# A two-block decoder on one core: PSUM split four and four, and seven-product first multiplications in four more expert layers

## The chip, the cores and the metric

The kernel runs on one core of one Trainium2 chip. The metric is device microseconds of one execution. Each kernel is timed in several runs; the profile is one more execution, taken by the hardware profiler. Engines are named as in the profile: PE multiplies matrices (PEld is its weight load), DVE, ACT and POOL work on vectors, SP starts most of the DMAs. PSUM, into which PE writes and which DVE and ACT read, has eight banks of 128 x 512 float32.

## The reference

Sixteen sequences of 128 rows of 256 features go through two blocks, all in float32. Every sublayer ends with `x = layernorm(x + sublayer(x))`.

```
block 0: causal attention, 16 heads of 64, over groups of 512 rows
         8 ensembles: o_e = relu(x @ in_e) @ out_e, summed with gates   (256 -> 512 -> 256)
         routed experts, best 2 of 16, and 2 shared ones
block 1: banded attention, 16 heads of 16
         cross attention to ctx_512, 16 heads of 16
         8 experts: y_e = gelu(x @ w1_e + b1_e) @ w2_e + b2_e, summed   (256 -> 512 -> 256)
```

In block 0 the gates of the eight ensembles come from an integer tensor and the context. In block 1 every expert works on every row, and the sum is scaled by one gate for each row. The change concerns the two layers of eight dense experts, which are called expert layers here, and where attention scores are put.

## The kernel before

**Groups.** The 16 sequences are worked in four groups of four, g = 0 to 3, of 512 rows each. A sublayer of one group is one stage, written as (number, g): 0 is causal attention (`attention0`), 1 the ensembles (`ensemble0`), 2 the routed experts (`experts0`, for two groups at once), 3 banded attention, 4 cross attention (both through `attention16`), 5 the dense experts of block 1 (`experts1`). There are eight expert layers: (1, 0) to (1, 3) and (5, 0) to (5, 3).

**Order of the work.** Every stage is a Python generator that emits instructions and yields an estimate of the PE time it has just emitted. The `Weaver` (L217 to L257) takes pieces from a main stream of attention stages and a side stream of dense stages, L1462, in shares given by hand (L1466 to L1472), with short streams for normalisation, gates, routing and loads in between. The first attention stages (0, 0) and (0, 1) run alone, then attention and experts run woven together, and the last two expert layers (5, 2) and (5, 3) run alone. A scheduler then orders instructions by that emission order as their operands and buffers come free, and gives every tile a buffer at build time; the program of each engine is fixed before it runs.

**PSUM.** `bank(tag)`, L49, takes a bank from one pool of six (tag "B"), whatever the tag in its name: psH, psM and psO in the profile all come from this pool. Attention scores, psS, have a tile of two banks of their own, tag "S" with one buffer (L424 in causal attention, L520 in the 16-head attention). In causal attention the DVE instruction L352 reads the scores once into SBUF. In banded attention L352 does too; in cross attention two DVE instructions read them from PSUM, L358 (the maximum) and L364 (its subtraction). The next scores wait until the last reader is done. After the softmax POOL multiplies by the reciprocal of the sum (L380), PE transposes (L60), ACT copies (L390), and PE multiplies with the values into psO.

**An expert layer.** `products` (L796) runs over nine steps. In step e the first products of expert e (`x @ in_e`, hidden layer of 512) are emitted in four pieces, and between them four pieces of the second products of expert e - 1. The second products always use the seven-product scheme for 2 x 2 blocks: four sums on DVE (L812 to L815), the blocks of the second weights summed by POOL beforehand (L696, L699) and kept in HBM, four banks psM and four additions into `acc` on DVE (L836).

**First products, plain.** A piece is one bank psH with two matmuls of 128 x 128 by 128 x 512 (`project`, L316), read by one instruction: L942 on DVE in block 0 (relu and gate), L1365 on ACT in block 1 (gelu and bias).

**First products by sevens** (class `Firsts`, L722), used before in (5, 2) and (5, 3) for experts 1 to 7. Expert 0 stays plain. Once for each layer DVE makes four block sums of the activations (`rows_sums`). For each expert POOL makes four sums of weight blocks, in place or in tag "cw" (`weight_sums`, L740, instructions L720 and L746). The seven products, 14 matmuls of 128 x 128 by 128 x 256, go partly into one running bank, `sums` (psH), which is read by ACT three times in between and keeps accumulating, and partly into `other` (psM):

```
            self.product(e, 5, sums)
            nc.scalar.copy(block(1, 0), sums)
            yield 0.91
            other = both(bank("M"))
            self.product(e, 4, sums)
            nc.scalar.copy(block(1, 1), sums)
            self.product(e, 3, other, start=True)
            added(1, 1, other)
            yield 1.82
            self.product(e, 2, other, stop=True)
            added(1, 0, other)
```

`added` is one DVE addition of 128 x 512 (L771); after it the block is finished by `done` (relu and gate, or two gelus).

**Tag "cw"** has four buffers, which `weight_sums` shares with the gate masks (L908, instruction L909), the routing plan and the collection of routed results (L1300).

Of the kernel before, what the change touches and what calls it, by code (L numbers as in the profile page):

```python
# [8 lines left out]
F32 = mybir.dt.float32  # L9
# [5 lines left out]
P = 128  # L15
D = 256
# [6 lines left out]
T = GB * P  # L23
# [8 lines left out]
def kernel(ctx: ExitStack, tc: tile.TileContext, a: dict, out: bass.AP):  # L32
# [11 lines left out]
    ps = ctx.enter_context(tc.tile_pool(name="psum", bufs=2, space=bass.MemoryType.PSUM))  # L44
# [2 lines left out]


    def bank(tag):  # L49
        return ps.tile([P, T], F32, tag="B", name=f"ps{tag}", bufs=6)  # L50

    recent = [None]

# [49 lines left out]
    def load_quad(j):  # L103

        cols = slice(j * D, (j + 1) * D)
        return load_w(
            "attn", 2048, f"wquad{j}", a["L0_attn_W_Q"][:, :, cols], a["L0_attn_W_K"][:, :, cols],
            a["L0_attn_W_V"][:, :, cols], a["L0_attn_W_O"][:, 2 * j:2 * j + 2, :],
        )
# [206 lines left out]
    def project(pt, w, cols, xT):  # L316

        for c in range(KC):
            mm(pt, lhsT=w[:, c, cols], rhs=xT[:, c, :], start=c == 0, stop=c == KC - 1)
# [76 lines left out]
    def attention0(x, g):  # L396
        norm = Norm(x)
        norm.bias(bo0)

        def project_quad(g, j):  # L400
            wq, wk, wv, wo = first_quads[j] if g == 0 and j < 2 else load_quad(j)
            xT = xTs[g]
            qT = p2.tile([P, 2, T], F32, tag="qT", name="qT")
            kT = p2.tile([P, 2, T], F32, tag="kT", name="kT")
            for i in range(2):
                c = 2 * j + i
                cols = slice(i * P, (i + 1) * P)
                pq = bank("H")
                project(pq, wq, cols, xT)
                nc.vector.tensor_scalar(  # L410
                    qT[:, i, :], pq, bq0[:, c:c + 1], 0.125, ALU.add, ALU.mult
                )
                pk = bank("H")
                project(pk, wk, cols, xT)
                nc.scalar.activation(kT[:, i, :], pk, AF.Identity, bias=bk0[:, c:c + 1])
                yield 3.44

            v = yield from values(xT, wv, KC)
            heads0[g, j] = qT, kT, v, wo

        def scores(j, b):
            qT, kT, _, _ = heads0[g, j]
            at = slice(b * P, (b + 1) * P)
            s = ps.tile([P, 2, T], F32, tag="S", name="psS", bufs=1)[:, :, :D].rearrange(  # L424
                "p s (i k) -> p s i k", i=2
            )

            for i in range(2):
                for k in range(2):
                    rows = slice(64 * k, 64 * k + 64)  # L430
                    with joined(i == k == 0):
                        mm(
                            s[:, k, i, :], lhsT=qT[rows, i, at], rhs=kT[rows, i, at],
                            start=True, stop=True,
                        )
            return softmax(s, causal)

        def output(j, b, zT):
            po = bank("H")[:, :D]
            for i in range(2):  # L440
                mm(po, lhsT=zT[:, i, :], rhs=heads0[g, j][3][:, i, :], start=i == 0, stop=i == 1)
            norm.add(b, po, last=j == 3)

        if (g, 0) not in heads0:
            yield from project_quad(g, 0)
        units = [(j, b) for j in range(4) for b in range(GB)]
        e, eT, zT, at = {}, {}, {}, {}
        for n in range(len(units) + 5):
            if n < 16:
                j, b = units[n]  # L450
                e[n] = scores(j, b)
                at["e", n] = weaver.now + 9.0
                yield 0.6
            m = n - 2
            if m in e:
                yield UNTIL, at["e", m]
                eT[m], _ = weights_T(e.pop(m))
                at["t", m] = weaver.now + 2.5
                yield 0.5
            m = n - 5  # L460
            if m in zT:
                yield UNTIL, at["z", m]
                output(*units[m], zT.pop(m))
                yield 0.86
            m = n - 4
            if m in eT:
                j, b = units[m]
                yield UNTIL, at["t", m]

                pz = bank("O")[:, :D].rearrange("p (c q) -> p c q", c=2)  # L470
                got = eT.pop(m)
                for i in range(2):
                    for k in range(2):
                        h = 2 * i + k
                        with joined(h == 0):
                            mm(
                                pz[64 * k:64 * k + 64, i, :],
                                lhsT=heads0[g, j][2][:, b, 64 * h:64 * h + 64],
                                rhs=got[:, 2 * k + i, :], start=True, stop=True,
                            )  # L480
                zT[m] = p3.tile([P, 2, P], F32, tag="z", name="zT")

                nc.vector.tensor_tensor(  # L483
                    zT[m], pz, bv0[:, 2 * j:2 * j + 2].unsqueeze(2).to_broadcast([P, 2, P]), ALU.add
                )
                at["z", m] = weaver.now + 2.5
                yield 0.6
            if n < 16 and (n < 12 or g + 1 < NG):

                j, b = units[n]  # L490
                if b == 0:
                    ahead = project_quad(g, j + 1) if j < 3 else project_quad(g + 1, 0)
                yield next(ahead)
                if b == 3:
                    assert next(ahead, None) is None
        assert not e and not eT and not zT
        norm.done()


    def attention16(x, qT, kT, v, bv, wo, bo, seen):  # L500
# [9 lines left out]
        def scores(b, c):  # L510

            at = slice(b * P, (b + 1) * P)

            kb = p2.tile([P, 4, P], F32, tag="kb", name="kb")
            nc.gpsimd.tensor_tensor(  # L515
                kb, kT[:, c, at].unsqueeze(1).to_broadcast([P, 4, P]),
                hm4.unsqueeze(2).to_broadcast([P, 4, P]), ALU.mult,
            )
            yield UNTIL, weaver.now + 2.0
            s = ps.tile([P, 2, T], F32, tag="S", name="psS", bufs=1)  # L520
            s = s[:, :, :4 * keys].rearrange("p s (h k) -> p s h k", h=4)
            for k in range(2):
                rows = slice(64 * k, 64 * k + 64)
                for queries, key, _ in parts:
                    mine = slice(b * P + queries.start, b * P + queries.stop)
                    with joined(k == 0 and key == 0):
                        mm(
                            s[queries, k], lhsT=qT[rows, c, mine],
                            rhs=kb[rows, :, key:key + keys], start=True, stop=True,
                        )  # L530
            return softmax(s, seen)
# [400 lines left out]
    def ensemble0(x, xT, g):  # L932
        def load(e):
            gt = p2.tile([P, T], F32, tag="sg", name="gt")
            nc.sync.dma_start(out=gt, in_=gates_of[g][e:e + 1, :].to_broadcast([P, T]))
            gates[e] = gt
            return load_up(f"we0_{e}", a["L0_xattn_proj_in"][e])[0]

        def hidden(h, up, e, c):
            ph = bank("H")  # L940
            project(ph, up, slice(c * P, (c + 1) * P), xT)
            nc.vector.scalar_tensor_tensor(  # L942
                out=h, in0=ph, scalar=0.0, in1=gates[e], op0=ALU.max, op1=ALU.mult
            )

        def done(to, got, e, i, j):
            gt = gates[e][:, j * 2 * P:(j + 1) * 2 * P]
            nc.vector.scalar_tensor_tensor(
                out=to, in0=got, scalar=0.0, in1=gt.unsqueeze(1).to_broadcast([P, 2, 2 * P]),
                op0=ALU.max, op1=ALU.mult,  # L950
            )

        gates = {}
        norm = Norm(x)
        yield from products(
            load, lambda e: load_blocks(0, e, g, a["L0_xattn_proj_out"][e]), hidden,
            lambda t: after(
                products_end(t, norm, None, lambda norm, b: norm.done(b, 2)), tail(1, g)
            ),
            Firsts(xT, done) if g in () else None,  # L960
        )

    def small(tag, n=16, bufs=None):
# [391 lines left out]
    def experts1(x, xT, g, ng):  # L1355
# [16 lines left out]
        for b in range(GB):  # L1372
# [4 lines left out]
        yield from products(  # L1377
            load, lambda e: load_blocks(1, e, g, a["L1_ffn_w2"][e]), hidden,
            lambda t: after(products_end(t, norm, ng, lambda norm, b: store(norm, g, b))),
            Firsts(xT, done) if g in (2,3) else None,  # L1380
        )


# [158 lines left out]
```

## Time and profile before

| | |
|---|---|
| time, median of 3 runs | 1738.57 us (1735.91 to 1738.95) |
| profiled execution, its own time | 1738.27 us |
| its span | 1736.6 us |
| mean granted PE clock | 0.975 |

The table shows busy us of each engine, in stretches cut at the ends of the expert layers (the last addition of a layer, L878, stands at 372.9, 538.9, 833.9, 1015.9, 1328.5, 1507.4, 1623.8 and 1721.9 us) and of the routed experts.

| from to, us | what runs | PE | DVE | ACT | POOL |
|---|---|---|---|---|---|
| 0 to 212 | (0, 0), (0, 1) | 203.1 | 117.6 | 93.0 | 96.5 |
| 212 to 539 | (1, 0), (1, 1) beside (0, 2), (0, 3) | 325.3 | 205.9 | 52.3 | 65.6 |
| 539 to 680 | routed experts, groups 0 and 1; rest of (0, 3) | 121.8 | 70.3 | 51.3 | 20.5 |
| 680 to 834 | (1, 2) beside attention | 150.9 | 123.8 | 24.6 | 46.3 |
| 834 to 1016 | (1, 3) beside attention | 176.6 | 152.2 | 40.6 | 52.3 |
| 1016 to 1150 | routed experts, groups 2 and 3, and attention | 114.4 | 86.2 | 52.4 | 44.1 |
| 1150 to 1328 | (5, 0) beside attention | 169.4 | 132.5 | 90.6 | 70.0 |
| 1328 to 1507 | (5, 1) beside attention | 173.8 | 131.9 | 93.0 | 56.6 |
| 1507 to 1736 | (5, 2), (5, 3) | 212.1 | 143.8 | 93.9 | 53.7 |

How to read it: matmuls are pipelined and the profile models their ends, so PE's busy time overstates what PE needs where passes overlap, and the start-to-start time of two records says what a pass costs. A float32 matmul stands as two records. Idle time of an engine that isn't the bound costs nothing. The slices of the page give the same picture over the span; each digit is a tenth of the slice:

```profile
PE   9999999999999799999899988998999999999996
...
DVE  4565565576677534878796875858769675965655
ACT  4434411111022242103131212643846372654342
POOL 5443532220002302312241315334224132522220
```

### The profile page before, as it was taken

What the parts mean: (1) busy time and instruction counts of PE and PEld (TensorE: products, weight loads), DVE (VectorE), ACT (ScalarE), POOL (GpSimd) and SP (SyncE); (2) the same over time, 40 slices, a digit from 0 to 9 for tenths busy, and PEclk for the clock granted to TensorE, in tenths of its full rate; (3) what the DMA queues carried; (4) which work ended last, traced back from release to release, by engine and by line L of the source; (5) the groups of instructions that cost most, each with busy time, mean ns of one, the idle gap of its engine ahead of it and who ended that gap; (6) DMA issues with size and microseconds to landing.
All of it is one profiled execution on the core that took longest, in us unless ns stands there. A gap on an engine that the chain in (4) does not pass through costs nothing.

```text
span 1736.6 us, 22830 instructions
## 1 busy us (share of the span) xinstructions
PE 1647.3 (95%) x8196; PEld 1080.5 (62%) x8196; DVE 1164.0 (67%) x2330; ACT 591.8 (34%) x1360; POOL 505.5 (29%) x543
## 2 busy tenths in 40 slices
PE   9999999999999799999899988998999999999996
PEld 6665656666656465656556655665665665588785
DVE  4565565576677534878796875858769675965655
ACT  4434411111022242103131212643846372654342
POOL 5443532220002302312241315334224132522220
PEclk9999999999998899999999989999999999999998
DMA  9533533432330458422223204671222221124330
GB/s 272 174 118 123 172 140 111 150 112 103 103 110 13 146 186 290 153 93 82 90 79 104 80 31 170 202 245 64 68 91 80 71 70 67 63 83 134 113 121 34
DMA packets 98192, 204.52 MB, mean 118 GB/s; under 512 B 16136, under 2 KB 58176, under 8 KB 98016
## 3 DMA queue, kind: packets, MB, share of 16 engines
q1 hardware_dynamic: 92176, 179.53, 31.2%
q0 software_dynamic: 5904, 23.54, 3.7%
q8 instruction: 65, 1.06, 0.2%
q14 instruction: 47, 0.39, 0.1%
HBM read 172.43 MB, written 37.81 MB: 121 GB/s over the span
## 4 chain that ended last, share of the span: by engine, by line
PE 75%; DVE 12%; DMA 4%; issue 3%; POOL 2%; ACT 1%; SPq 1%; another core or an unknown queue 0%; POOLq 0%; DVEq 0%; ACTq 0%
PE psH L55 40%; PE psM L55 21%; PE psO L60 5%; PE psS L55 4%; PE psO L55 3%; PE psH L60 2%; DVE nmax L358 1%; DVE e L364 1%; DMA wquad<-in_L_attn_W_Q 1%; DMA rows<-copies 1%; DVE total L370 1%; DVE x L311 1%; DVE x L293 1%; DVE acc L836 1%; POOL got L1303 1%
## 5 line engine op out<-in xcount | busy, mean ns | idle before, releaser
L55 PE MATMUL psH<-xT,we 128*128 128x512 f32 (+1 forms) x856 | 397.4, 590 | 0.5 <-DMA we<-in_L_xattn_proj_in 0.5
L380 POOL TENSOR_TENSOR e<-e,inv 128x512 f32<-128x512 f32 (+2 forms) x121 | 159.4, 1319 | 425.6 <-DVE inv L378 369.7
L55 PE MATMUL psM<-cm,wb 128*128 128x256 f32 x1024 | 263.6, 381 | 0.0
L55 PEld LDWEIGHTS psH<-xT,we 128*128 128x128 f32 x856 | 156.8, 191 | 137.0 <-issue 124.9
L55 PEld LDWEIGHTS psM<-cm,wb 128*128 128x128 f32 x1024 | 192.0, 190 | 52.2 <-issue 25.7
L55 PE MATMUL psM<-h,wb 128*128 128x256 f32 x768 | 200.8, 384 | 5.0 <-ACT h L1365 3.4
L836 DVE TENSOR_TENSOR acc<-psM,acc 128x512 f32<-128x512 f32 (+1 forms) x216 | 134.5, 624 | 98.3 <-PE psM L55 98.2
L390 ACT COPY eT<-psO 128x512 f32<-128x512 f32 (+1 forms) x192 | 105.5, 584 | 275.6 <-PE psO L60 261.3
L55 PEld LDWEIGHTS psM<-h,wb 128*128 128x128 f32 x768 | 143.0, 190 | 54.8 <-issue 29.3
L373 ACT ACTIVATE e<-e,nmax 128x128 f32<-128x128 f32 x256 | 99.5, 390 | 139.6 <-DVE nmax L358 113.4
L942 DVE SCALAR_TENSOR_TENSOR h<-psH,gt 128x512 f32<-128x512 f32 x128 | 87.6, 685 | 71.5 <-PE psH L55 71.2
L55 PE MATMUL psH<-xT,wquad 128*128 128x512 f32 x256 | 117.2, 601 | 6.1 <-DMA wquad<-in_L_attn_W_Q 5.4
L515 POOL TENSOR_TENSOR kb<-kT,hm 128x512 f32<-128x512 f32 x64 | 72.4, 1134 | 159.1 <-PE psS L55 104.5
L60 PEld LDWEIGHTS psO<-ident,e 128*128 128x128 f32 (+1 forms) x768 | 85.2, 133 | 48.2 <-issue 35.9
L60 PE MATMUL psO<-ident,e 128*128 128x128 f32 (+1 forms) x768 | 109.7, 280 | 2.0 <-POOL e L380 2.0
L1365 ACT ACTIVATE h<-psH,b 128x512 f32<-128x512 f32 (+1 forms) x100 | 60.6, 623 | 104.7 <-PE psH L55 95.9
L369 ACT ACTIVATE e<-e 128x576 f32<-128x576 f32 (+1 forms) x64 | 55.7, 871 | 88.2 <-DVE e L364 87.9
L55 PEld LDWEIGHTS psH<-xT,wquad 128*128 128x128 f32 x256 | 46.7, 190 | 58.9 <-issue 47.8
L309 POOL TENSOR_TENSOR rstd<-ve,mhalf 128x4 f32<-128x4 f32 (+1 forms) x32 | 28.9, 903 | 177.9 <-DVE ve L307 177.6
L370 DVE TENSOR_REDUCE total<-e 128x8 f32<-128x576 f32 (+1 forms) x64 | 62.8, 981 | 24.6 <-ACT e L369 24.0
L55 PE MATMUL psO<-eT,v 128*64 128x128 f32 (+2 forms) x1024 | 76.6, 313 | 0.0
L55 PE MATMUL psH<-wquad,zT 128*128 128x256 f32 x256 | 67.8, 388 | 4.8 <-DVE zT L483 2.5
(240 smaller groups left out, 2624.0 us busy)
## 6 DMA issues: line engine op xcount, KB each, us to landing
wb<-wbd SPq DMA_DIRECT2D x56, 896.0 KB
we<-in_L_xattn_proj_in SPq DMA_DIRECT2D x32, 512.0 KB
wt<-table SPq DMA_DIRECT2D x64, 256.0 KB
we<-in_L_ffn_w SPq DMA_DIRECT2D x32, 512.0 KB
wbd<-wb POOLq DMA_DIRECT2D x16, 896.0 KB
gt<-gatesd SPq DMA_DIRECT2D x32, 256.0 KB
results<-y SPq DMA_DIRECT2D x10, 768.0 KB
rows<-copies SPq DMA_DIRECT2D x6, 1024.0 KB
```

The source lines that it names most:

```text
L55: recent[0] = nc.tensor.matmul(*args, **how)
L60: return nc.tensor.transpose(out_, in_, ident[:n, :n])
L309: nc.gpsimd.tensor_tensor(rstd[:, at], ve[:, at], mhalf[:, at], ALU.pow)
L369: nc.scalar.activation(e, e, AF.Exp)
L370: nc.vector.tensor_reduce(total, e, AX.X, ALU.add)
L373: nc.scalar.activation(e[:, h, :], s[:, h // (n // 2), h % (n // 2), :], AF.Exp, bias=nmax[:, h:h + 1], accum_out=total[:, h:h + 1],)
L380: engine.tensor_tensor(e, e, inv.unsqueeze(2).to_broadcast([P, n, keys]), ALU.mult)
L390: return eT, nc.scalar.copy(eT, pt)
L515: nc.gpsimd.tensor_tensor(kb, kT[:, c, at].unsqueeze(1).to_broadcast([P, 4, P]), hm4.unsqueeze(2).to_broadcast([P, 4, P]), ALU.mult,)
L836: nc.vector.tensor_tensor(to, pm[:, :len(slots), :], to, ALU.add)
L942: nc.vector.scalar_tensor_tensor(out=h, in0=ph, scalar=0.0, in1=gates[e], op0=ALU.max, op1=ALU.mult)
L1365: nc.scalar.activation(to, one, AF.Gelu, bias=b1[:, 4 * e + c:4 * e + c + 1])
```

## The change

Three numbers and two lists. The pool "B" has four banks where it had six. The scores' tag "S" has two buffers of two banks where it had one. `Firsts` is used in (1, 0), (1, 1) and (1, 3), where block 0 had it nowhere, and in (5, 1) beside (5, 2) and (5, 3). (1, 2) and (5, 0) stay plain. Everything else is as before, the numbers that guide the weaver included, but a step by sevens yields 1.82, 0.91, 1.82 and 1.82 where four plain pieces yield 1.72 each.

```diff
     def bank(tag):
-        return ps.tile([P, T], F32, tag="B", name=f"ps{tag}", bufs=6)
+        return ps.tile([P, T], F32, tag="B", name=f"ps{tag}", bufs=4)
...
         def scores(j, b):
-            s = ps.tile([P, 2, T], F32, tag="S", name="psS", bufs=1)[:, :, :D].rearrange(
+            s = ps.tile([P, 2, T], F32, tag="S", name="psS", bufs=2)[:, :, :D].rearrange(
...
             yield UNTIL, weaver.now + 2.0
-            s = ps.tile([P, 2, T], F32, tag="S", name="psS", bufs=1)
+            s = ps.tile([P, 2, T], F32, tag="S", name="psS", bufs=2)
...
-            Firsts(xT, done) if g in () else None,
+            Firsts(xT, done) if g in (0,1,3) else None,
...
-            Firsts(xT, done) if g in (2,3) else None,
+            Firsts(xT, done) if g in (1,2,3) else None,
```

## The prediction

> **What bounds the kernel now.** I read the page's busy shares first, then the table of stages, then PE's waits, then the timeline at four places.
>
> ```profile
> PE 1647.3 (95%) x8196; PEld 1080.5 (62%) x8196; DVE 1164.0 (67%) x2330; ACT 591.8 (34%) x1360; POOL 505.5 (29%) x543
> ```
>
> Over the whole span PE is the bound and DVE has a third of its time free. The stage table corrects that average. Its columns are stretch, length, then busy us of PE, PEld, DVE, ACT, POOL. The four stretches are the four expert layers that the change converts, cut where each layer's last addition (L878) stands: first block groups 0, 1 and 3, then second block group 1.
>
> ```profile
> 212.00:373.00 161.00, 159.29 (x648) 99.14 (x647) 96.37 (x168) 24.03 (x82) 50.34 (x75) 1.00 0.39 137
> 373.00:539.00 166.00, 166.00 (x734) 106.17 (x732) 109.52 (x225) 28.28 (x101) 15.30 (x16) 1.00 0.29 95
> 834.00:1016.00 182.00, 176.60 (x881) 108.48 (x880) 152.16 (x288) 40.61 (x71) 52.27 (x41) 0.98 0.23 79
> 1328.00:1507.00 179.00, 173.76 (x873) 105.94 (x874) 131.87 (x241) 93.01 (x126) 56.62 (x48) 0.99 0.20 68
> ```
>
> In the first two, PE is full and DVE is at 60 and 66%. In the third DVE is at 84%, in the fourth at 74%. Cut into 20 us pieces, the third and fourth show that DVE is full exactly where the 16-head attention runs beside the experts:
>
> ```profile
> 874.00:894.00 20.00, 20.00 (x96) 11.57 (x94) 19.15 (x28) 7.19 (x11) 8.49 (x6) 1.00 0.26 86
> 894.00:914.00 20.00, 19.98 (x110) 11.79 (x112) 19.68 (x31) 7.95 (x13) 6.96 (x4) 1.00 0.25 86
> 974.00:994.00 20.00, 20.00 (x146) 12.36 (x145) 19.32 (x35) 7.30 (x14) 8.56 (x7) 1.00 0.22 73
> 1488.00:1507.00 19.00, 18.22 (x102) 11.27 (x102) 18.93 (x31) 10.70 (x15) 12.93 (x12) 1.00 0.31 104
> ```
>
> So two places have one bound (PE), two have two bounds at once (PE and DVE). In PE's list of waits the single scores set is the only PSUM buffer that shows as such; what ends those waits is the DVE instruction that reads the old scores:
>
> ```profile
> PE psS L55 <- DVE e L352: 7.7, 7, 2.2
> ...
> PE psS L55 <- DVE e L364: 3.9, 4, 1.8
> ```
>
> **First products by sevens, on PE: -24.1 us.** Each product is two records. Plain, an expert's first products are 16 records of 512 columns; by sevens they are 14 products of 256 columns, 28 records. What a record costs is start to start, from the timeline of a plain layer and of group 2 of the second block, which already works by sevens:
>
> ```profile
> 288.31 1.88 PE L55 MATMUL psH<-xT,we 128*128 128x512 f32 x4
> ...
> 290.03 0.59 PE L55 MATMUL psM<-h,wb 128*128 128x256 f32 x2
> ```
> ```profile
> 1560.16 1.89 PE L55 MATMUL psM<-cm,wb 128*128 128x256 f32 x8
> 1561.88 1.03 PE L55 MATMUL psM<-tx,we 128*128 128x256 f32 x4
> ```
>
> 1.72 us for four of 512 (0.43 each), 1.72 us for eight of 256 (0.215 each). 16 x 0.43 = 6.88; 28 x 0.215 = 6.02; 0.86 us saved per expert, 7 experts of 8 (the first stays plain), 6.0 per layer, 24.1 for four. The Trainium skill, "Perfetto Trace Analysis", section Optimizing Tensor Performance, speaks against it: larger matmuls are more efficient than smaller ones. By that rule part of the 24.1 would be lost to twice the weight loads and shorter passes. By the rows nothing is: half the columns take half the time, and the weight loads (0.19 us) hide under them. I keep 24.1.
>
> **What it adds elsewhere, per converted expert.** DVE: three additions at L771 of 0.69 us = 2.07; the rectifying instructions or activations keep their elements. ACT: three copies of 0.59 = 1.76 (and, in the second block, eight activations of 0.5 for four of 0.69, +1.2). POOL: four weight sums of 0.73 = 2.9, in POOL's queue ahead of attention's normalisations (L380) and key masks (L515). Once per layer four row sums of 0.42 on DVE. Number and bytes of the DMAs stay; SP's queue is passed by nothing. POOL's sums also hinder DVE: while POOL multiplied at L380 from 900.46 to 902.36, this DVE addition of two SBUF tiles took 2.38 us where 0.69 is usual:
>
> ```profile
> 900.52 2.38 DVE L813 TENSOR_TENSOR cm<-h 128x512 f32<-128x512 f32 x1
> ```
>
> An expert takes some 22 us here; 2.9 us of POOL is 13% of it. An expert has seven DVE instructions with both inputs in SBUF, so one of them is hit, for about half of 0.73: +0.4. DVE gains 2.07 + 0.4 = 2.47 us per expert.
>
> Groups 0 and 1 of the first block: DVE goes from 96 and 110 us to about 115 and 129 of 155 and 160, so it stays hidden under PE. I charge 1.5 us each, +3, for sums that come late where gates (L909) hold the four buffers of tag "cw" that the weight sums also use, and for PE waiting on a copy (between 0 and 5 each).
>
> First block, group 3: the full pieces (874 to 914, 974 to 1016) last 82 us with DVE 77.7. At 22.75 us per expert they hold 3.6 experts: 77.7 + 3.6 x 2.47 = 86.6, so DVE sets them, +4.6. The other 3.4 experts give PE's 0.86 each, -2.9. Net +1.7 in place of -6.0: correction +7.7.
>
> Second block, group 1: the full pieces (1328 to 1348, 1408 to 1428, 1468 to 1507) last 79 us with DVE 73.0, and hold 3.5 experts: 81.6, +2.6; the rest -3.0. Net -0.4: correction +5.6.
>
> **Second scores set: -5.6 us.** PE's waits on the set are 7.7 + 3.9 + 0.2 = 11.8 us in 12 places. In the other hundred-odd places the set had been free before the next scores, mostly for over 1 us. Of the 11.8, 3.5 lie before 212 us and 2.1 between 539 and 680, where DVE has room: those go, 5.6. The other 6.2 are like this one, in pieces where DVE is full; the wait ends, and PE waits next for the instructions that DVE runs later instead:
>
> ```profile
> 1471.57 1.21 DVE L364 TENSOR_TENSOR e<-psS,nmax 128x1024 f32<-128x1024 f32 x1
> ...
> 1472.92 0.70 PE L55 MATMUL psS<-kb,qT 64*128 64x512 f32 x2 [1.80 <-DVE e L364]
> ```
>
> Bounds: 0 and 11.8.
>
> **Six banks become four: +7 us.** Counting in the timeline from each bank's first matmul to the end of its last reader, 1.6 banks are in use on average in the first two stages, 2.0 to 2.5 later. The skill (same page, Matmul Optimizations and Optimizing Tensor Performance) wants all eight banks used and groups rotated through them, so that reading one overlaps filling the next; by that rule a third less rotation costs everywhere. By the count it costs only where more than four are in use: no time to speak of before 539, but in the stages that stay plain 7.0 us (539 to 680), 4.7 (680 to 834), 6.3 (1016 to 1150) and 10.9 (1150 to 1328), 28.9 in all. Behind a matmul that waits for a bank stands all of PE, scores included, and behind those DVE's own next work. Bounds: 0 (PE had run ahead of DVE and loses nothing) and 28.9. I take a quarter, 7: PE's waits on the scores set, the nearest row, average 1 us each, and these excesses come in 44 pieces of 0.7 us, of which much is PE running ahead.
>
> **Sum.** -24.1 + 3 + 7.7 + 5.6 - 5.6 + 7 = -6.4 against the profiled execution's own 1738.27 us (span 1736.6): 1731.9. That execution is 0.3 us from the median 1738.57, so no correction.
>
> **Rivals.** (1) Everything is hidden: DVE's backlog in the full pieces is worked off in the next ones and no bank is missed. -24.1 - 5.6 = 1708.6; with the +3, 1711.6. For it: ACT and POOL are under 55% everywhere, and the layers by sevens alone run at 12.08 us per expert, which is 56 x 0.216, without a gap. Against it: DVE at 96 to 98% in three quoted pieces.
>
> (2) Slower: banks run out. By sevens one bank (the running sum) is held from an expert's first product to its last, and a second between products 3 and 2, so the rest share two or three. In the four converted stages more than three are in use for 2.5, 2.7, 9.4 and 20.8 us, 35.4; with the 28.9 above, 64.3 us of shortage. Without any bank cost the sum stands at -13.4; so the change turns slower once PE stands for over 13.4 us, 21% of it. At two fifths, 25.7: 1750.6. Late DVE instructions in the group 3 and second-block stages are where it would show.
>
> (3) The second set does nothing and the later conversions cost more than DVE's sum says, so that it ends within 0.2% of before, which is about what a measurement can tell from no change: 1738.
>
> **How the numbers follow.** Likeliest (0.42): 1732, own range 1723 to 1740. Rival 1: 0.25. Rivals 2 and 3: 0.27 and 0.06. Faster by over 0.2% (below 1735): 0.27 of the likeliest and all of rival 1, 0.52. Slower: rival 2 and 0.05 of the likeliest, 0.32. Same: 0.16. The range takes in rival 1 and most of rival 2: 1709 to 1756.
>
> **What would show it.** Right: the stretches to the first two L878 marks are each 4 to 6 us shorter with PE still full; the group 3 layer is as long as before with DVE over 95%; waits on psS gone before 680. Rival 2: PE's list of waits names psH, psM or psO ended by DVE or ACT readers, in tens of us. Wrong altogether: if the order of work on PE is drawn up differently, so that stages shift against each other, and if weight sums on POOL delay attention's L380.

## The result, and the profile after

| | before | after |
|---|---|---|
| median of 5 runs each, same chip | 1738.95 us (1735.91 to 1742.33) | 1750.38 us (1746.61 to 1751.9) |
| ratio to before | | 1.0059 [1.0044, 1.0074] |
| profiled execution, its own time | 1738.27 us | 1746.61 us |
| its span | 1736.6 us | 1744.6 us |

The kernel became 0.6% slower. The forecast was 0.4% faster. 1750 is inside the range and next to the number of rival 2.

The page's busy shares after the change. Each engine stands with its busy us, its share of the span and its instructions:

```profile
PE 1638.8 (94%) x8532; PEld 1145.1 (66%) x8532; DVE 1220.7 (70%) x2431; ACT 636.9 (37%) x1466; POOL 598.4 (34%) x654
```

PE has 336 records more, 12 for each of 28 experts, as 28 in place of 16 should give. It is busy for less time, and the span is longer, so the new time is time in which PE stands.

The table of stages after the change, columns as before: stretch, length, busy us of PE, PEld, DVE, ACT, POOL. The rows are the four converted layers, cut again at their last L878:

```profile
208.00:364.00 156.00, 155.08 (x723) 114.58 (x722) 109.62 (x190) 35.71 (x103) 79.34 (x111) 1.00 0.41 142
364.00:522.00 158.00, 157.64 (x804) 120.29 (x803) 123.37 (x242) 37.49 (x112) 32.82 (x35) 1.00 0.30 99
818.00:1001.00 183.00, 173.42 (x957) 121.78 (x955) 162.32 (x301) 49.42 (x86) 66.34 (x59) 1.00 0.25 81
1320.00:1502.00 182.00, 173.34 (x954) 122.57 (x955) 138.89 (x259) 104.42 (x172) 70.84 (x67) 0.97 0.21 69
```

The first two layers do what was forecast: they are shorter and PE is still full. The layer ends come at 364.1 and 522.3 us, where they stood at 372.9 and 538.9. So the kernel is 16.6 us ahead when the routed experts begin. That is more than the first products explain: some 4 us of PE's other work now stand later. The third row is as long as before, as forecast, but DVE is at 89% in it (162.3 of 183 us) and not over 95%. The fourth is 3 us longer, and PE is less full in the third than it was.

PE's list of waits after the change. These are the rows for the scores set and the largest rows in which a bank of the shared pool can be what is waited for (engine, tile and line that wait, what ends the wait, us in all, times, longest):

```profile
PE psH L60 <- DVE acc L836: 2.8, 2, 2.4
PE psM L55 <- DVE acc L836: 2.5, 3, 1.8
PE psS L55 <- DVE e L352: 2.0, 5, 0.4
PE psM L55 <- DVE h L771: 1.7, 3, 0.8
PE psM L55 <- ACT eT L390: 1.5, 2, 0.9
...
PE psO L55 <- ACT h L1365: 1.2, 2, 0.6
PE psO L60 <- DVE h L771: 1.2, 2, 0.6
...
PE psS L55 <- DVE e L364: 0.6, 1, 0.6
```

The scores waits are down from 11.6 us (two rows) to 2.6. In their place stand rows that did not exist before: a product into one kind of bank waits for the reader of another kind. `psO` needs nothing from `h` at L771 or L1365; it waits because three names, psH, psM and psO, draw on four banks. All rows in which psH, psM or psO wait for an instruction at L390, L771, L834, L836, L942 or L1365 make 17.9 us. Before, the only one was this:

```profile
PE psM L55 <- ACT h L1365: 3.4, 3, 2.7
```

A row in which psM waits for `h` can be a wait for data, as the second products read `h`. Without such rows it is 15.6 us after and nothing before.

**A measure of lost time.** From the trace of before I took the time from start to start that each kind of PE record has when nothing is in its way. I summed it over a stretch, and call the rest of the stretch lost. The level depends on the times chosen for the smallest products; differences between kernels depend on them by 1 or 2 us only. Before, PE's records need 1478.1 us; after, 1455.0. That is 23.1 less, where 24.1 was forecast. As the times are those of before, this figure can't tell whether the shorter passes lose anything. The lost time in us by stretch, which is my own working from the traces:

| stretch, ends at L878 marks | before | after | difference |
|---|---|---|---|
| start to the end of (1, 1) | 58.9 | 58.0 | -0.9 |
| routed experts and (1, 2) | 57.3 | 57.5 | +0.2 |
| (1, 3) | 25.4 | 32.3 | +6.9 |
| routed experts and (5, 0) | 68.4 | 78.9 | +10.5 |
| (5, 1) | 25.0 | 32.2 | +7.2 |
| (5, 2) | 6.1 | 13.5 | +7.4 |
| (5, 3) | 4.1 | 3.6 | -0.5 |

The lost time grew by 31 us, nearly all of it after 818 us. The two stretches with routed experts differ between traces and chips by several us. The others repeat within 2 us in sum: before has 119.5 and 117.4 in two traces. So the sums below are over those others, and called lost outside the routed stretches.

### The profile page after: what moved, and what is told of

It is laid out like the page before. It is cut to its first block, busy times and chain, and to the rows that moved or that the text cites. A ratio compares the mean times of both kernels' runs of the same rounds, so it can differ in the third digit from the quotient of the medians.

```text
span 1744.6 us, 23960 instructions
## 1 busy us (share of the span) xinstructions
PE 1638.8 (94%) x8532; PEld 1145.1 (66%) x8532; DVE 1220.7 (70%) x2431; ACT 636.9 (37%) x1466; POOL 598.4 (34%) x654
## 4 chain that ended last, share of the span: by engine, by line
PE 70%; DVE 16%; DMA 4%; issue 3%; POOL 3%; ACT 2%; another core or an unknown queue 1%; SPq 0%; POOLq 0%; DVEq 0%; ACTq 0%
PE psH L55 35%; PE psM L55 24%; PE psO L60 4%; PE psO L55 3%; PE psS L55 3%; DVE e L364 2%; PE psH L60 2%; DVE nmax L358 2%; DVE total L370 1%; DVE acc L836 1%; DMA rows<-copies 1%; DMA wquad<-in_L_attn_W_Q 1%; DVE e L352 1%; DVE x L311 1%
## 5 line engine op out<-in xcount | busy, mean ns | idle before, releaser
L55 PEld LDWEIGHTS psM<-cm,wb 128*128 128x128 f32 x1024 | 191.4, 190 | 47.1 <-issue 13.7
L55 PE MATMUL psH<-xT,we 128*128 128x512 f32 (+1 forms) x520 | 209.8, 531 | 1.5 <-DVE h L942 0.9
L836 DVE TENSOR_TENSOR acc<-psM,acc 128x512 f32<-128x512 f32 (+1 forms) x216 | 134.4, 624 | 88.9 <-PE psM L55 88.4
L390 ACT COPY eT<-psO 128x512 f32<-128x512 f32 (+1 forms) x192 | 107.3, 582 | 181.7 <-PE psO L60 163.2
L55 PEld LDWEIGHTS psH<-xT,we 128*128 128x128 f32 x520 | 95.6, 190 | 72.4 <-issue 57.2
L720 POOL TENSOR_TENSOR sw<-we 128x256 f32<-128x256 f32 x84 | 66.9, 797 | 173.3 <-PE psM L55 114.8
L60 PE MATMUL psO<-ident,e 128*128 128x128 f32 (+1 forms) x768 | 113.9, 283 | 5.8 <-issue 2.5
L771 DVE TENSOR_TENSOR h<-psM,h 128x512 f32<-128x512 f32 x126 | 86.5, 686 | 44.4 <-PE psM L55 41.0
L515 POOL TENSOR_TENSOR kb<-kT,hm 128x512 f32<-128x512 f32 x64 | 71.5, 1120 | 127.8 <-PE psS L55 96.2
L1365 ACT ACTIVATE h<-h,b 128x256 f32<-128x256 f32 x126 | 57.1, 500 | 60.9 <-DVE h L771 60.8
L1365 ACT ACTIVATE h<-psH,b 128x512 f32<-128x512 f32 (+1 forms) x86 | 47.9, 576 | 79.3 <-PE psH L55 70.0
```

Source lines behind the costliest of these rows:

```text
L55: recent[0] = nc.tensor.matmul(*args, **how)
L60: return nc.tensor.transpose(out_, in_, ident[:n, :n])
L390: return eT, nc.scalar.copy(eT, pt)
L515: nc.gpsimd.tensor_tensor(kb, kT[:, c, at].unsqueeze(1).to_broadcast([P, 4, P]), hm4.unsqueeze(2).to_broadcast([P, 4, P]), ALU.mult,)
L720: engine.tensor_tensor(to, one, two, ALU.subtract)
L771: nc.vector.tensor_tensor(block(i, j), other, block(i, j), ALU.add)
```

## The experiments

Each kernel was compared with before on its own chip. The chips differ. The median of before was 1728.09, 1740.19, 1728.86, 1726.77 and 1740.23 us in the five groups of runs, so times are compared through their ratio to before, and a figure in us is the ratio's difference times that median. There are two kinds of chips: the first, third and fourth group ran on one where before takes about 1728 us, the second and fifth, like the result, on one where it takes about 1740. The fifth group shows that even ratios differ between the kinds, by up to half a per cent. Every edit changes only the numbers of the diff, but for the two kernels of the third group.

### First group: the split alone, the sevens alone

Two theories: the smaller pool costs more than the forecast's +7 (A), or the conversions cost more than their sums (B).

```diff
-        return ps.tile([P, T], F32, tag="B", name=f"ps{tag}", bufs=6)
+        return ps.tile([P, T], F32, tag="B", name=f"ps{tag}", bufs=4)
...
-            s = ps.tile([P, 2, T], F32, tag="S", name="psS", bufs=1)
+            s = ps.tile([P, 2, T], F32, tag="S", name="psS", bufs=2)
```

Four banks and two sets, no new layer by sevens:

> PSUM split four and four with two score sets, first products as before (by sevens in the last two layers alone). Theory A (the bank pool is what was mis-sized: four banks cost PE far more than 7 us in the stages woven with attention): the scores set gives back about 5 us, four banks cost about 20 us, so 1750 to 1756 us. Theory B (the conversions are what was mis-sized: the added DVE, ACT and POOL work delays attention, also in stages that stay plain): the split alone costs what the prediction had, 7 minus 5.6, so 1737 to 1742 us.

Measured: 1.0078 [1.0059, 1.0097], 13.5 us.

The other half of the diff alone, six banks and one set, all four layers:

```diff
-            Firsts(xT, done) if g in () else None,
+            Firsts(xT, done) if g in (0,1,3) else None,
...
-            Firsts(xT, done) if g in (2,3) else None,
+            Firsts(xT, done) if g in (1,2,3) else None,
```

> First products by sevens in the four more layers, PSUM as before (six banks, one score set). Theory A: 24 us of PE work saved, some 13 given back to DVE in the two later layers, 3 in the two early ones: 1729 to 1733 us. Theory B: the lost time comes with the conversions, so 24 saved and some 30 to 36 lost: 1745 to 1752 us.

Measured: 0.9962 [0.9948, 0.9976], 6.6 us less, as theory A had it.

The same with `(0,1)` and `(2,3)`, the early two layers alone:

> By sevens in the first two layers of block 0 besides the last two of block 1, PSUM as before. Both theories have DVE free there: 12 us saved, 3 lost, 1728 to 1732 us. If it is not faster, the prediction's step on the two early layers is wrong too, or the gain is given back later where the stages shift against each other.

Measured: 0.9938 [0.9919, 0.9958], 10.7 us less.

Four banks, one set (`bufs=4` and `bufs=1`), no new layer:

> Four banks in the pool and one score set (two banks of PSUM unused), first products as before. Against the run with the split alone it prices the second score set, against before it prices the loss of two banks. Theory A: 1755 to 1762 us. Theory B: about 7 us over before, 1743 to 1748 us. Both: 4 to 8 us above the run with the split alone.

Measured: 1.0127 [1.0108, 1.0145], 22 us. So the loss of two banks costs 22 us where layers are plain, and the second set gives back 0.5%, 8.5 us. The split as a whole is a loss of 13.5 us, where the forecast's own two terms make +1.4. A holds on this chip. Here is PE in the trace of the kernel with four banks and one set:

```profile
PE psS L55 <- DVE e L352: 4.7, 6, 0.9
...
PE psH L60 <- DVE h L942: 4.1, 2, 3.9
...
PE psM L55 <- DVE acc L836: 3.6, 3, 2.6
```

The bank waits stand there without any new conversion: without psM on `h`, such rows make some 15 us, none before. The timeline of the same kernel shows how one looks; the columns are start, us, engine, line, what is done, count, and in brackets the idle time before it with its releaser:

```profile
900.88 1.04 PE L60 MATMUL psO<-ident,e 128*128 128x128 f32 x8
902.24 0.64 PE L55 MATMUL psO<-eT,v 128*32 128x256 f32 x8 [0.32 <-DVE h L942]
...
1506.62 1.03 PE L55 MATMUL psH<-wx,zT 128*128 128x256 f32 x4
1508.59 0.64 PE L55 MATMUL psO<-eT,v 128*32 128x256 f32 x8 [0.93 <-DVE acc L836]
```

The product of probabilities and values reads `eT` and `v`. What released it, by the trace, is an instruction of an expert whose result it doesn't read, and which empties a bank. The program of PE has a fixed order, so what stands behind such a product waits these 0.3 to 0.9 us too. In the first two layers four banks cost nothing: they end at 372.7 and 538.8 us here, at 372.9 and 538.9 before.

### Second group: how many banks, which layers

The first kernel is before once more, for a trace of this chip:

> The kernel before, unchanged, for a profile from the chip of the neighbouring runs. Both theories: its own time, no difference.

Measured: 1736.34 us, one run.

Five banks, one set, no new layer (`bufs=5`):

> Five banks in the pool, one score set, first products as before. If four banks cost by shortage, as counted in the timeline of before (28.9 us with more than four banks in use, but only some 3 us with more than five), the fifth bank takes back most of the 20 us that four cost: 0 to 6 us over before. If the cost comes from the order of work being drawn up anew and not from shortage, five may cost as much as four: 10 to 20 us over.

Measured: 1.0005 [0.9992, 1.0019]. The sixth bank is worth nothing here. The fifth would then be worth 1.2%, but the 1.0127 of four banks comes from a chip of the other kind. That is a threshold, as the counting in the forecast has it: time with more than five banks in use is a few us in all in the timeline of before, with more than four some 40 us.

Four banks, two sets, the early two layers by sevens:

> Four and four with two score sets, by sevens only in the first two layers of block 0 and the last two of block 1. Theory A with costs that add up: 12 to 13 us saved as with six banks, 13 lost to the split: within 3 us of before. If held banks make the shortage worse in the early layers: 5 to 8 us over.

Measured: 0.9993 [0.9982, 1.0004], 1 us less than before, as costs that add up have it.

Six banks, one set, the early two and (5, 1), with `(0,1)` and `(1,2,3)`:

> Six banks and one set, by sevens in groups 0 and 1 of block 0 and groups 1, 2, 3 of block 1. The prediction's step for block 1, group 1, had it at -0.4 us net: the same as with the early ones alone, 11 to 13 us under before. If the second-block conversion is what lost most of the 5 us between the early ones alone and all four, it is 8 us under before or less, and the group 3 layer is innocent.

Measured: 0.993 [0.9914, 0.9946], 1728.39 against 1740.19 us. This is faster than both kernels of the case. With (1, 3) added it is the kernel of the first group that stood, on a chip of the other kind, at 0.9962. The trace of the kernel without (1, 3), stages (1, 3) and (5, 1):

```profile
821.00:997.60 176.60, 170.21 (x854) 105.23 (x852) 148.48 (x280) 37.48 (x65) 51.22 (x39) 1.00 0.24 80
1307.00:1479.20 172.20, 164.97 (x937) 120.59 (x938) 134.06 (x254) 100.44 (x166) 67.96 (x65) 1.00 0.22 73
```

and of the kernel with all four, six banks:

```profile
815.70:993.60 177.90, 167.53 (x945) 121.95 (x944) 161.03 (x301) 48.80 (x87) 67.53 (x59) 0.99 0.23 78
1300.00:1482.40 182.40, 172.12 (x961) 123.94 (x960) 139.56 (x258) 102.67 (x171) 71.10 (x67) 0.98 0.21 69
```

Converting (1, 3) makes its own stage 1.7 us longer (176.1 and 177.8 between the marks to a tenth), which is the forecast's net +1.7. It makes (5, 1), which is by sevens in both, 10 us longer, of which 8 are lost time (24.9 and 32.9). (5, 2) gives 2.8 of lost time back (13.7 and 10.9). Here a conversion is paid for two layers later. That is not a rule: in the fourth group's kernel without the early two layers, (1, 3) itself takes 187.3 us and (5, 1) 169.7.

### Third group: what the group 3 conversion costs

Theory: DVE's additions, or POOL's sums beside them, make (1, 3) dear, and the DVE share of a stage says what a conversion costs. In the first kernel the weight sums of (1, 3) are left out:

```diff
+            if self.drop == 'sums':
+                self.w[e] = a00, a01, a11, a10, a10, a00, a01
+                return
```

> The four layers by sevens with six banks and one score set, but in the group 3 layer of block 0 POOL's four weight sums per expert are left out (the products take unsummed blocks, so that layer's values are wrong). Same PE and DVE instructions. With all four layers the ratio to before was 0.996, without group 3 0.993. If POOL is what makes group 3 lose (its port, or its queue ahead of the normalisations), the ratio falls to 0.993 or below; if DVE's additions are, it stays at 0.995 to 0.997.

Measured: 0.9955 [0.9938, 0.9972]. In the second the additions L771 of (1, 3) are left out:

```diff
-                nc.vector.tensor_tensor(block(i, j), other, block(i, j), ALU.add)
+                if self.drop != 'adds':
+                    nc.vector.tensor_tensor(block(i, j), other, block(i, j), ALU.add)
```

> The same, but in the group 3 layer DVE's three additions per expert (14.5 us in all) are left out and POOL's sums stay (that layer's values are wrong). If DVE's added work makes group 3 lose, the ratio to before falls to 0.990 to 0.993; if POOL does, it stays at 0.995 to 0.997.

Measured: 0.9954 [0.9936, 0.9971]. Neither differs from 0.9962 by more than the intervals, which are 3 us wide to either side. The stages tell more. This is (1, 3) without the additions:

```profile
806.50:982.10 175.60, 165.49 (x942) 121.75 (x940) 153.13 (x280) 49.26 (x86) 67.52 (x59) 1.00 0.24 79
```

It takes 175.6 us where it took 177.8, so the additions cost 2 us there, with DVE at 87% in place of 91. (5, 1) takes 183.7 where it took 182.3, and (5, 2) 128.2 where it took 127.8. The edit also leaves each expert's two banks `other` unread, so that they come free sooner, and not all of the 2 us need be DVE's. Without the weight sums (1, 3) takes 181.2 us, which is longer and not shorter.

The best kernel with one more layer, (5, 0), where DVE is at 74%:

> Six banks, one set, by sevens in groups 0 and 1 of block 0 and all four of block 1. The added layer (block 1, group 0) has DVE at 74% over its stage, like group 1, whose conversion gave about 1 us. If DVE's share of the stage decides: within 3 us of the run with groups 1, 2, 3 of block 1, ratio 0.991 to 0.995. If held banks decide (this stage had most time with over four banks in use): ratio 0.996 or above.

Measured: 0.9984 [0.997, 0.9997], where the best kernel had 0.993 on a chip of the other kind. And with (1, 2), DVE at 80%, in place of (5, 0):

> Six banks, one set, by sevens in groups 0, 1, 2 of block 0 and 1, 2, 3 of block 1. The added layer has DVE at 80% of its stage and full in part of it. If DVE's share decides, it loses as group 3 did, some 3 to 6 us: ratio 0.995 to 0.997. Otherwise 0.991 or below.

Measured: 1.0014 [1.0001, 1.0027]. On this same chip the kernels with (1, 3), at 84%, stood at 0.9955 and 0.9954, with some of its work left out that changed nothing measurable. So (5, 0) and (1, 2), with more room on DVE, cost 0.3% and 0.6% more than (1, 3). The DVE share of a stage does not order the prices, and this theory falls.

### Fourth group: does the smaller pool make conversions dearer?

Rival 2 had a second half: by sevens an expert holds a running bank, so the shortage grows. The two late conversions are made with four banks and with six, on one chip.

> Four banks in two sets as in the change, no new layer by sevens; the base line of this comparison. Measured before on another chip at 1.0078 of before [1.0059, 1.0097]. Both theories expect that again, 1.007 to 1.009.

Measured: 1.0087 [1.007, 1.0104], the first group's 1.0078 again.

> Four banks in two sets, and by sevens only the two layers where DVE is full: (1, 3) and (5, 1). Theory P (the price of the smaller pool is the same whether a layer is plain or by sevens): the conversion costs what it costs with six banks, about +0.24%, so 1.010 of before. Theory Q (rival 2's second half: the running sum that is held through an expert makes the shortage worse): +0.6% or more, so 1.014 or above.

Measured: 1.012 [1.0101, 1.0139], 0.33% above the split alone. This lies between the theories' 1.010 and 1.014.

> The same two layers by sevens with six banks and one set. Both theories: the difference of the two earlier kernels with six banks (all four layers 0.9962, early two 0.9938), so 1.002 to 1.003 of before. It is what d2 less d1 is compared with.

Measured: 1.0058 [1.0042, 1.0075]. With six banks the same conversions cost 0.58%, not less than with four. So Q falls for four banks. The figure misses both theories' 1.002 to 1.003 too: the late two alone cost 10 us, and on top of the early two 4 us (0.9938 to 0.9962). Without the early two, (1, 3) loses 37.4 us; with them 29.9. This pair of kernels also shows where the split costs, as both convert the same layers on one chip: the stretches that end with (5, 0), (5, 1) and (5, 2) are 8.5, 5.5 and 5.7 us longer with four banks and two sets, and all that comes earlier is 11.6 us shorter.

> All four layers by sevens with five banks and one set. Theory P: five banks cost nothing, as in the plain layers (1.0005), so 0.996 to 0.997. Theory Q: with one bank held by the running sum five banks are as short as four in the converted layers, some part of the 1.2% that the fifth bank cost, so 0.999 or above.

Measured: 1.0007 [0.9995, 1.0019], where theory P had 0.996 to 0.997. This speaks for Q with five banks, unless the chips differ.

### Fifth group: chip or bank

> All four layers by sevens with four banks and one set. Theory P (the fifth bank costs 1.2% as in the plain layers, whatever the layers are): against five banks with all four (1.0007) that is 1.012 to 1.013. Theory Q (the running sum takes a bank out of the pool, so the shortage is larger with every size of the pool): 1.016 or above. The second set would then be worth the rest to the change's 1.0059: about 0.6% by P (0.5% in the plain layers), 1.0% or more by Q.

Measured: 1.0093 [1.007, 1.0117]. This is less than either theory had, as both reckoned from the 1.0007 of another chip.

> All four layers by sevens with six banks and one set, again, beside the above on one chip. 0.996 as on the other chip, if the 0.45% between it and five banks with all four comes of the bank and not of the chip; 1.000 if of the chip.

Measured: 1.0011 [0.9998, 1.0023], for the same program that stood at 0.9962. So chips alone move this ratio by 0.5%. In its trace here, the routed experts with the rest of (0, 3), (1, 2), then (1, 3) and (5, 1):

```profile
525.90:670.00 144.10, 123.11 (x680) 82.59 (x679) 72.47 (x205) 53.63 (x179) 20.84 (x21) 0.92 0.48 157
670.00:825.80 155.80, 152.29 (x736) 94.68 (x735) 128.20 (x241) 22.80 (x47) 54.30 (x49) 0.99 0.40 133
825.80:1003.60 177.80, 167.43 (x945) 121.86 (x944) 160.94 (x300) 48.72 (x86) 67.49 (x59) 0.99 0.24 78
...
1317.10:1499.40 182.30, 172.21 (x961) 124.02 (x959) 138.58 (x257) 102.57 (x171) 71.09 (x67) 0.98 0.21 69
```

(1, 3) and (5, 1) take the same 177.8 and 182.3 us as on the other chip. From the end of (1, 1) to the end of (1, 2) it is 299.9 us here and 291.7 there, from the end of (1, 3) to the end of (5, 0) 313.5 and 306.5. These two make 15.2 of the 17.0 us by which the spans differ, and the traces show what happens in them. Here is an ACT instruction of banded attention after the routed experts of groups 2 and 3 have begun, and the product behind it, first on this chip, then in the changed kernel. The third row is ACT on the other chip:

```profile
1059.54 0.62 ACT L554 ACTIVATE hz<-psO,even 128x128 f32<-128x128 f32 x2 [15.11 <-remote]
1060.34 2.07 PE L55 MATMUL psH<-wa,zT 128*128 128x256 f32 x4 [6.67 <-DVE zT L559]
```
```profile
1054.79 0.62 ACT L554 ACTIVATE hz<-psO,even 128x128 f32<-128x128 f32 x2 [15.11 <-remote]
1055.59 1.22 PE L55 MATMUL psH<-wa,zT 128*128 128x256 f32 x2 [6.67 <-DVE zT L559]
```
```profile
1035.37 0.74 ACT L554 ACTIVATE hz<-psO,even 128x128 f32<-128x128 f32 x2 [2.65 <-PE psO L55]
```

"remote" says that the profile knows nothing that ended the wait. ACT stands for 15.1 us, most of them while POOL issues the copies of rows for the routed experts (L1127), and DVE and PE wait behind it. Such stops of DVE or ACT are in all eight traces from chips where before takes about 1740 us, and only in the two stretches with routed experts. None of the twelve traces from chips where it takes about 1728 us has one. What stops the engines is open.

The 1.0007 of five banks is not explained by this, as its chip is of the kind on which six banks stood at 0.9962; the split alone reads 1.0078 and 1.0087 on these two chips. Outside the routed stretches five banks lose 139.9 us, six 137.2 and 139.0. But PE's waits with five banks and all four layers have rows like these:

```profile
PE psO L55 <- DVE acc L836: 2.8, 2, 2.0
...
PE psH L55 <- DVE acc L836: 2.3, 2, 1.5
```

Without psM on `h` they make 8.9 us, where five banks with plain layers have 1.8 and six banks with all four by sevens 1.7 and 2.5. So theory Q is not settled for five banks.

Four banks instead of six, both with one set, cost 0.82% (14 us) with all four layers by sevens, and 1.27% (22 us) with plain ones, on chips of the two kinds. Lost time outside the routed stretches, in us (two numbers are two chips or traces):

| banks, sets | no new layer | all four by sevens |
|---|---|---|
| 6, 1 | 119.5, 117.4 | 137.2, 139.0 |
| 5, 1 | 118.6 | 139.9 |
| 4, 1 | 131.3 | 148.2 |
| 4, 2 | 123.2, 122.4 | 139.6 |

Down each column the fifth bank is worth 12.7 and 8.3 us, the second set 8.5 and 8.6. Across, the conversions lose 16 to 22 us with any pool. So with four banks the two halves of the change add up, and the held running sum makes nothing worse. With banks free of charge the conversions would not have reached the forecast on every chip either.

## Why the prediction was wrong

- **PE, -24.1.** Right: 23.1 less by the base times, and the shorter passes keep theirs. In the first two layers after the change the median record of 256 columns in the first products takes 0.216 us from start to start. The rule about larger matmuls that the forecast weighed did not bind; the rows decided.
- **Early two layers, +3.** Right as a whole: -9 forecast, and the ratio 0.9938 is 10.7 us. In the changed kernel the two stages lose 3.2 us more (9.3 and 9.8 before, 11.0 and 11.3 after), the size of the +3. Its two reasons are not shown: in PE's list of waits for these stages neither a copy nor a weight sum stands. What the sum left out is far from them: with the early two alone, (5, 2) loses 11.8 where it lost 6.1, because the experts now run ahead and more of the last cross attention falls beside (5, 2): 16 records of its scores stand behind the end of (5, 1), where 4 stood.
- **(1, 3) and (5, 1), +7.7 and +5.6.** The +1.7 of (1, 3) came out in its own stage, but that was luck: the forecast had DVE's added work make 7.7 us of it, and leaving the additions out saves 2. For (5, 1) it had -0.4 us. With (1, 3) plain, the stage of (5, 1) falls from 178.8 us to 172.1, as if PE alone counted; the pieces that the forecast called full had DVE at 92% (73.0 of 79 us). With (1, 3) by sevens as well it takes 182.3. **This step failed too:** the sum gives each layer's price in its own stage and has no term for what a converted layer does to other stages, 8 us of lost time in (5, 1) and what the routed stretches make of it. By ratios, adding (1, 3) costs 0.8% (0.993 to 1.0011) on two chips of the result's kind, where +1.7 us, 0.1%, was forecast; the 0.9962 of a chip of the other kind would make it 0.3%.
- **Weight sums on POOL, DVE hindered by +0.4 per expert.** Not seen: DVE's 32 sums of two SBUF tiles in (1, 3), L812 to L815, take 24.4 us in all with the weight sums and 24.4 without. The ratios, 0.9962 and 0.9955, could hardly have shown 3 us.
- **Second scores set, -5.6.** Right, somewhat small: 8.5 us with plain layers. More of the waits where DVE is full were real gains than the forecast allowed: of 5.6 us before 680 us 2.0 remain after the change, of the 6.2 behind it 0.6.
- **"Six banks become four: +7 us."** This step failed, by its size. The runs put 14 to 22 us in its place. The forecast counted the shortage of four stretches only, 28.9 us, and took a quarter, because PE's other PSUM waits were short and PE was thought to run ahead. But in the stages that it left out, (1, 3), (5, 1) and (5, 2), four banks with one set lost 12.6 us more than before (in (1, 3) 28.1 for 25.4, in (5, 1) 31.4 for 25.0, in (5, 2) 9.6 for 6.1). And with the 8.7 us of shortage that the plain (5, 1) has, which were not in the 28.9, and some 2 us elsewhere, the count is 39.7 us; 22 is over half of it. That PE runs ahead and loses nothing is not borne out. The reading that fits, argued and not isolated, is that PE's program has a fixed order, so that a matmul that waits for a bank holds scores and transposes on which DVE's next work hangs.

What each term did on chips of the result's kind: the conversions +1.9 us where the sum had -7.8, the loss of two banks +14.3 for +7 (both from the fifth group), and the second set -5.9 for -5.6 (the change against four banks and one set, on two chips). Together that is 10.3 us, the result's 0.59%. So the miss of 16.7 us has two parts, 9.7 from the conversions and 7.3 from the banks. On the first group's chip nearly all of it would be the banks: -6.6 for -7.8, and +13.5 for the +1.4 of the split.

Rival 2 was right in its first half: banks run out, and the waits that it named stand in the list, 15.6 to 17.9 us of them. That its 1750.6 is next to the result is luck. It had 25.7 us for the banks and -13.4 for all else; on chips of the result's kind the runs have 14.3 and -4.0. Its second half, the running sum that makes the shortage worse, did not show with four banks.

Taken together for the profiled executions: -23.1 of PE work, +20.1 lost outside the routed stretches and +10.7 in them give +7.7, and the spans differ by 8.0. Of the 10.7 the wait of 6.7 us behind ACT's stop is not banks, as six banks have it too, and before has no stop of ACT there. How the rest divides can't be told: before has no trace on the chip where all four ran with six banks, and the stops make these stretches repeat only within several us. Why a converted (1, 3) costs (5, 1) 8 us is also not isolated. The scheduler orders the work anew when one layer changes, so every later stage differs in what falls beside what; that is argued, not shown.

## What to carry to other kernels

Count buffers in use over time before taking any away, in every stage and not only in the ones that the change leaves alone; here the price was nil down to five with plain layers, and over half of the counted shortage at four. When an engine's program is written ahead in a fixed order, don't discount a wait for a buffer to a quarter because another engine seems to be behind. In a kernel woven from several streams, test each converted layer by itself and on more than one chip. The lowest ratio, 0.993, is that of six banks with (1, 0), (1, 1) and (5, 1) converted; the first two alone, at 0.9938 on a chip of the other kind, can't be told from it.

## What was not expected of the hardware

One program had the ratio 0.9962 on one chip and 1.0011 on another, each give or take 0.0014. The stages without routed experts agreed to 0.1 us in (1, 3) and (5, 1), and the two stretches with them differed by 8.2 and 7.0 us. Before itself stood at 1727 to 1729 us on three chips and at 1739 to 1740 on three others, the result's among them. Only on these does the profile show ACT or DVE standing for up to 15 us, for a reason that it doesn't name, and a change of order moves the stops. A ratio of this kernel from one chip is thus no property of the program alone to better than half a per cent.
